# Group statistics by 32x32 transpositions and one aggregation on VectorE instead of two small TensorE products

## The chip, the cores and the metric

The kernel runs on one core of one Trainium2 chip. The metric is the device time of one execution in microseconds (us). Engines are named as in the profile: PE is TensorE's matrix product, PEld its weight load, DVE is VectorE, ACT is ScalarE, POOL is GpSimd, SP is SyncE (here it only issues transfers).

## The reference

An attention block over 16 images of 512 channels by 32x32 pixels, all in float32: a group normalisation, query, key and value products, softmax attention with four heads, an output product and the residual.

```python
b, c, h, w = x.shape                        # 16, 512, 32, 32
xg = x.reshape(b, NUM_GROUPS, -1)           # 8 groups of 64 channels
mu = jnp.mean(xg, axis=-1, keepdims=True)
var = jnp.var(xg, axis=-1, keepdims=True)
xn = ((xg - mu) * jax.lax.rsqrt(var + EPS)).reshape(b, c, h, w)
xn = xn * norm_gamma[:, None, None] + norm_beta[:, None, None]
qkv = jnp.einsum('oc,bchw->bohw', qkv_w, xn) + qkv_b[:, None, None]
q, k, v = jnp.split(qkv, 3, axis=1)         # then to 4 heads of 128
attn = jax.nn.softmax(jnp.einsum('bhnd,bhmd->bhnm', q, k) * scale, axis=-1)
out = jnp.einsum('bhnm,bhmd->bhnd', attn, v)
out = jnp.einsum('oc,bchw->bohw', proj_w, out) + proj_b[:, None, None]
return x + out
```

## The kernel before

Channels lie on the 128 partitions: an image is four tiles `x` (chunks c = 0 to 3) of 128 x 1024 numbers, and a group of 64 channels is half of the partitions of one chunk. The attention runs as one long sequence of steps, eight per head, four heads per image. In each step TensorE makes scores (L846, tile `s`), ScalarE their exponentials (L852, `p`), VectorE adds the exponentials up (L858, L860, `tot`), and TensorE makes the weighted sum of the step before (L942, `po`).

All other work is planned between these steps by `plan_head`, a list of units for each of the eight steps of a head: the query and key products of the next image, the value products, and the output product of the image before, all by Strassen's scheme on two levels (`strassen`, `two_levels`, tiles `qk_*`, `v_*`, `pp_*`). Its products go to PSUM banks x and y of the pool `ps_a`, two of each. Bank x is emptied by copies on ScalarE (L486, L628; `pp_p`, `pp_u`), bank y by additions on VectorE (L630; `pp_r`), and TensorE can only go on in a bank that has been emptied. Sums of inputs for the inner level are VectorE's (L574, `pp_t`; L319 for the image's own sums), as are the combinations of results (L679, 1024 wide), the residual additions (L826, L829, `y`) and the division by the softmax sum (L952). POOL issues the transfers of `x`, of the residual `y` and of the output `out_y` (L830). A scheduler puts the instructions of the units into one fixed order for each engine; `tc.issue_after` and `tc.high_priority(URGENT)` steer it.

The normalisation of image b + 1 is prepared while head 1 of image b runs. `load_x` brings the four chunks. `stats_chunk`, on ScalarE, makes the mean and the variance of each channel (columns 0 and 1 of `mv`). `stats_group` makes the statistics of the groups from these, four columns for the four chunks: a product with the matrix `avg` (blocks of 64 x 64 filled with 1/64) spreads the groups' mean of the channels' means over the partitions (L83, `pm`), VectorE makes the deviation's square and adds the variances, a second product spreads the group's variance (L88, `pv`), VectorE adds epsilon (L89, `ve`), POOL raises to the power -0.5 (L90, `rstd`), and VectorE multiplies by gamma and makes the shift (L76, L100, L102; `sc`, `t`, `sh`). The three parts are pinned behind the additions to `tot` of steps 2, 3 and 4 (3 for the first such image). Then `normalise` (L109 on ScalarE) scales and shifts the image in halves of a chunk. In PSUM `pm` and `pv` take a bank y each. Image 0 is prepared in `open_image`, in two pairs of chunks.

The tile with the tag `tt` has one buffer; the squares' output of `stats_chunk` (`junk`) and the transposed sums of `denominators` share it.

Of the kernel before, what the change touches and what calls it, by code (L numbers as in the profile page):

```python
# [10 lines left out]
F32 = mybir.dt.float32  # L11
I32 = mybir.dt.int32
AF = mybir.ActivationFunctionType
ALU = mybir.AluOpType
AX = mybir.AxisListType

P = 128
HEADS = 4
GROUPS = 8
EPS = 1e-5  # L20
BLK = 32
# [6 lines left out]
URGENT = 40  # L28
# [158 lines left out]
def fast_path(ctx, tc, x, sources, out, consts, flag, dims):  # L187
# [6 lines left out]
    nc = tc.nc  # L194
    B, C, N, NCC, NH2, NB, GC, SCALE = dims
    gamma, beta, qkv_wT, qk_b, v_b, proj_wT, proj_b = sources
    avg, neghalf, gamma_sb, beta_sb, qkb_sb, vb_sb, projb_sb = consts
# [4 lines left out]
    one = ctx.enter_context(tc.tile_pool(name="one", bufs=1))  # L202
# [8 lines left out]
    lpool = ctx.enter_context(tc.tile_pool(name="l", bufs=1))  # L211
    upool = ctx.enter_context(tc.tile_pool(name="u", bufs=2))
    ypool = ctx.enter_context(tc.tile_pool(name="y", bufs=4))
    gn = ctx.enter_context(tc.tile_pool(name="gn", bufs=2))
# [7 lines left out]
    spans = one.tile([BLK, B * HEADS - 1], F32, name="spans")  # L222
    ones = one.tile([BLK, 1], F32, name="ones")
    ones_sq = one.tile([P, P], F32, name="ones_sq")
    xs, xb, vs, qs, ks, os_, ob = {}, {}, {}, {}, {}, {}, {}
    mvs, scaled = {}, {}

# [20 lines left out]
        nc.vector.memset(avg[ts(g, GC), ts(g, GC)], 1.0 / GC)  # L248
    nc.vector.memset(neghalf, -0.5)
    nc.vector.memset(ones_sq, 1.0)  # L250
    for t, src in (
        (gamma_sb, gamma), (beta_sb, beta), (qkb_sb, qk_b), (vb_sb, v_b), (projb_sb, proj_b)
    ):
        nc.gpsimd.dma_start(t, src)

    norm = Norm(nc, gn, ps_a, avg, neghalf, gamma_sb, beta_sb, NCC, N, "y")

    def stats_chunk(b, c):
        if c == 0:
            mvs[b] = gn.tile([P, NCC, 2], F32, tag="mv", name=f"mv_{b}")  # L260

        junk = lpool.tile([P, N], F32, tag="tt", name=f"junk_{b}_{c}")
        sums = gn.tile([P, 3], F32, tag="st", name=f"sums_{b}_{c}")
        nc.scalar.activation(junk, xs[b, c], AF.Identity, accum_out=sums[:, 0:1])
        nc.scalar.mul(mvs[b][:, c, 0:1], sums[:, 0:1], 1.0 / N)
        nc.scalar.mul(sums[:, 1:2], sums[:, 0:1], -1.0 / N)
        nc.scalar.activation(
            junk, xs[b, c], AF.Square, bias=sums[:, 1:2], accum_out=sums[:, 2:3]
        )
        nc.scalar.mul(mvs[b][:, c, 1:2], sums[:, 2:3], 1.0 / N)  # L270

    def stats_group(b):


        g = []

        def part(n, first, last):
            if not g:
                g.extend(norm.group_steps(mvs[b]))
            with tc.issue_after(added[b - 1, 1, n].ins), tc.high_priority(URGENT):  # L280
                for step in g[first:last]:
                    step()

        def scale():
            n = 4 if b > 1 else 3
            part(n, 9, 10)
            with tc.issue_after(added[b - 1, 1, n].ins), tc.high_priority(URGENT):
                mu, sc = norm.result
                sh = norm.shift(mu, sc)
            for c in range(NCC):  # L290
                scaled[b, c] = sc, sh, c

        return [lambda: part(2, 0, 6), lambda: part(3, 6, 9), scale]

    def normalise(b, c, half, on_scalar=True):
        t = xs[b, c][:, ts(half, HALF)]
        sc, sh, i = scaled[b, c]
        return norm.apply(t, t, sc, sh, i, on_scalar)
# [16 lines left out]
    def sums_of_b(b, rows=(1, 2, 3), chunks=range(KC)):  # L315

        def sub(o, i, j):
            for k in chunks:
                nc.vector.tensor_sub(b[o][k], b[i][k], b[j][k])  # L319

        if 1 in rows:
            sub("t1", "b12", "b11")
        if 2 in rows:
            sub("t2", "b22", "t1")
        if 3 in rows:
            sub("t3", "t2", "b11")
            sub("t4", "b21", "t2")

    def x_sums(b, rows=(1, 2, 3)):
        if 1 in rows:  # L330
            xb[b] = halves([xs[b, c] for c in range(NCC)], "x")
        sums_of_b(xb[b], rows)

    def o_blocks(b):
        ob[b] = halves([os_[b, h] for h in range(HEADS)], "o")
# [33 lines left out]
    def stage_blocks(site):  # L369

        raw = raw_blocks(site)
        st = stage[site] = {}
        names = ("a11", "a12", "a21", "a22", "s1", "s2")
        if site in ("proj", "v"):
            for n in names[:4]:
                st[n] = ypool.tile([P, HALF], F32, tag="y", name=f"st_{n}")
            for i, n in enumerate(names[4:]):
                st[n] = tpool.tile([P, HALF], F32, tag=f"ot2{i}", name=f"st_{n}")
        else:
            for i in range(3):  # L380
                t = opool.tile([P, N], F32, tag="o", name=f"st_{site}_{i}")
                for h in range(2):
                    st[names[2 * i + h]] = t[:, ts(h, HALF)]
        for n in names[:4]:
            load_block(st[n].rearrange("p (s d) -> p s d", d=P), raw[n])
# [450 lines left out]
    inverse, rows_of, added, exps = {}, {}, {}, {}  # L836
    steps = B * HEADS * NB
# [116 lines left out]
    def spread(plan, units, first, last):  # L954

        for i, u in enumerate(units):
            plan[first + i * (last - first) // len(units)].append(u)
# [20 lines left out]
    def staggered(lists, starts=None):  # L978


        starts = starts or (0, 4, 8, 16)[: len(lists)]
        at = [(a + i, g, u) for g, (a, us) in enumerate(zip(starts, lists))
              for i, u in enumerate(us)]
        return [u for _, _, u in sorted(at, key=lambda t: t[:2])]
# [104 lines left out]
    def plan_head(b, h):  # L1089

        plan = [[] for _ in range(NB)]
        if h == 0:
            spread(plan, staggered(next_qk.pop()), 0, NB)
            if b > 0:
                plan[6].append(lambda: o_blocks(b - 1))
                plan[6].append(lambda: sums_of_b(ob[b - 1]))
            else:
                plan[5].append(lambda: stage_blocks("v"))
        elif h == 1:
            if b > 0:  # L1100
                spread(plan, staggered(proj_groups(b - 1)), 0, NB)
            if b + 1 == B:
                plan[0].append(lambda: last_loads("x"))
            else:
                plan[0].append(lambda: load_x(b + 1))
                spread(plan, [lambda c=c: stats_chunk(b + 1, c) for c in range(NCC)], 2, 4)
                sums, power, scale = stats_group(b + 1)
                if b == 0:

                    plan[4] += [sums, power, scale]  # L1110
                else:
                    plan[4].insert(0, sums)
                    plan[4].insert((len(plan[4]) + 1) // 2, power)
                    plan[5].insert(0, scale)
                for r in range(2):
                    plan[5 + r] += [

                        lambda c=c, half=half: normalise(b + 1, c, half, b > 0 or c % 2 == 1)
                        for c in range(KC * r, KC * r + KC) for half in range(NH2)
                    ]  # L1120
                plan[6].append(lambda: x_sums(b + 1, (1,)))
            if b == 0:
                for g in range(len(OUTER)):
                    plan[g // 2].append(lambda g=g: kept_group("v", g))
                    plan[NB // 2 - 1 + g].append(lambda g=g: kept_group("proj", g))
                plan[2].append(lambda: stage_blocks("proj"))
                spread(plan, [lambda o=o: bias_of_v(o) for o in range(NCC)], 3, 5)
        elif b + 1 == B:
            if h == 2:
                plan[0].append(lambda: last_loads("w"))  # L1130
                plan[2].append(last_bias)
            else:
                os_[b, h] = opool.tile([P, N], F32, tag="o", name=f"o_{b}_{h}")
                plan[3].append(lambda: o_blocks(b))
                plan[3].append(lambda: sums_of_b(ob[b], (1,)))
                plan[5].append(lambda: sums_of_b(ob[b], (2, 3), (0,)))
        elif h == 2:
            spread(plan, staggered(qk_groups(b + 1, 0)), 0, NB)

            plan[0].insert(2, lambda: x_sums(b + 1, (2,)))  # L1140
            plan[1].append(lambda: x_sums(b + 1, (3,)))
        else:

            spread(plan, staggered(next_v.pop()), 0, NB - 1)

            plan[NB - 2].append(lambda: ahead[f"qk_{b + 1}_1"]())
        return plan
# [92 lines left out]
    plan = []  # L1240
    for s in range(steps + 1):
        units = []
        if s < steps:
            b, h, j = where(s)
            if j == 0:
                plan = plan_head(b, h)
# [7 lines left out]
        for half in range(NH2):  # L1254
# [11 lines left out]
            n = (len(units) + 1) // 2  # L1266
# [137 lines left out]
```

## Time and profile before

| | |
|---|---|
| Median of three runs | 3172.76 us (3171.57 to 3177.14) |
| Profiled execution, span | 3170.7 us |
| Around the span, against the median | 2.1 us |
| Granted TensorE clock | 1.000 |
| PE, DVE, ACT, POOL busy | 3159.9, 2633.6, 1439.7, 517.7 us |
| `pm` and `pv`, 128x4 | 30 TensorE passes each (two for one float32 product) |
| Power on POOL (L90), 128x4 | 15, mean 1940 ns |

How to read it: a float32 product is two records (passes) of TensorE. A record's length exceeds the spacing of the starts since passes overlap, so lengths of time on TensorE are read from start to start. A line of the timeline gives start, length, engine, source line, operation, tiles, shapes and the number of instructions merged; in brackets stands the engine's idle time before it and what ended it. In a line of a group, the numbers after the count are the busy time in us and the mean of one in ns. The word "now" in the prediction means the kernel before.

### The profile page before, as it was taken

How to read it: one execution, taken by the hardware profiler on the slowest of the kernel's cores; microseconds unless marked ns; L12 is line 12 of the kernel's file. 1: busy time of each engine (PE TensorE's matmuls, PEld its weight loads, DVE VectorE, ACT ScalarE, POOL GpSimd, SP SyncE). 2: the span in 40 equal slices, each digit the busy share in tenths (PEclk: the TensorE clock that was granted, in tenths of full speed). 3: DMA queues.
4: the chain of work that ended last, by engine and by line, in shares of the span. 5: the costliest groups of instructions: out<-in, count | busy, mean ns of one | idle time of the engine just before them, and what ended most of it. 6: DMA issues, size and time to landing. Idle time of an engine off the chain costs nothing.

```text
span 3170.7 us, 34267 instructions
## 1 busy us (share of the span) xinstructions
PE 3159.9 (100%) x10524; PEld 2190.7 (69%) x10524; DVE 2633.6 (83%) x4639; ACT 1439.7 (45%) x2712; POOL 517.7 (16%) x898
## 2 busy tenths in 40 slices
PE   9999999999999999999999999999999999999999
PEld 7566676677766676777767767677676776766764
DVE  9878879788897888878788787987879978788784
ACT  3535435354353543545435453453534545344342
POOL 0011221111211112211122111222012221122200
PEclk9999999999999999999999999999999999999999
DMA  5554554555545455454554545555455564555531
GB/s 177 185 190 154 188 172 154 171 153 192 171 164 162 153 185 175 167 167 145 191 172 162 171 145 187 171 172 172 144 175 169 176 189 134 174 162 186 179 116 41
DMA packets 210333, 524.32 MB, mean 165 GB/s; under 512 B 32096, under 2 KB 65376, under 8 KB 210144
## 3 DMA queue, kind: packets, MB, share of 16 engines
q1 hardware_dynamic: 132896, 282.12, 28.8%
q0 software_dynamic: 64000, 204.54, 19.2%
q10 hardware_dynamic: 13248, 35.39, 3.5%
q8 instruction: 87, 1.43, 0.2%
q14 instruction: 102, 0.84, 0.1%
HBM read 388.77 MB, written 133.17 MB: 165 GB/s over the span
## 4 chain that ended last, share of the span: by engine, by line
PE 96%; DVE 3%; DMA 0%; issue 0%; POOL 0%; SPq 0%; ACT 0%; DVEq 0%; POOLq 0%
PE po L942 27%; PE s L846 27%; PE qk_x L606 12%; PE qk_y L606 9%; PE pp_x L606 6%; PE v_x L606 6%; PE pp_y L606 4%; PE v_y L606 4%; PE lx L1031 0%; DVE qk_t L574 0%; PE ly L1031 0%; PE warm L1153 0%; DVE tot L860 0%; DVE qk L714 0%; DVE qk_r L630 0%
## 5 line engine op out<-in xcount | busy, mean ns | idle before, releaser
L942 PE MATMUL po<-p,v 128*128 128x512 f32 x2048 | 1049.5, 594 | 0.7 <-ACT p L852 0.7
L846 PE MATMUL s<-qk,qk 128*128 128x512 f32 x2048 | 1047.4, 593 | 0.3 <-DVE qk L714 0.3
L852 ACT ACTIVATE p<-s 128x512 f32<-128x512 f32 x1024 | 610.9, 597 | 961.0 <-PE s L846 957.2
L942 PEld LDWEIGHTS po<-p,v 128*128 128x128 f32 x2048 | 603.6, 302 | 322.7 <-issue 214.5
L860 DVE TENSOR_TENSOR tot<-tot,p 128x1024 f32<-128x1024 f32 x385 | 469.0, 1218 | 158.4 <-ACT p L852 156.3
L846 PEld LDWEIGHTS s<-qk,qk 128*128 128x128 f32 x2048 | 387.7, 190 | 88.6 <-issue 29.9
L606 PEld LDWEIGHTS qk_x<-qk_t,w 128*128 128x128 f32 x1344 | 251.8, 190 | 166.1 <-issue 75.3
L606 PE MATMUL qk_x<-qk_t,w 128*128 128x256 f32 x1344 | 356.3, 382 | 0.1
L486 ACT COPY qk_u<-qk_x 128x512 f32<-128x512 f32 (+1 forms) x256 | 136.3, 533 | 229.2 <-PE qk_x L606 229.2
L779 POOL DMA_DIRECT2D vd<-vu x120 | 66.7, 557 | 899.8 <-DVE vu L771 897.9
L630 DVE TENSOR_TENSOR qk_r<-qk_y,qk_u 128x512 f32<-128x512 f32 (+1 forms) x256 | 157.7, 616 | 34.7 <-ACT qk_u L486 21.6
L580 POOL DMA_DIRECT2D kept_t<-qk_t x240 | 129.4, 540 | 278.4 <-DVE qk_t L574 211.9
L606 PEld LDWEIGHTS pp_x<-pp_t,w_proj 128*128 128x128 f32 x630 | 117.2, 190 | 74.7 <-issue 32.3
L784 POOL DMA_DIRECT2D v<-vd x240 | 140.6, 593 | 167.1 <-DMA vd<-vu 70.3
L630 DVE TENSOR_TENSOR v_r<-v_y,v_u 128x512 f32<-128x512 f32 (+1 forms) x120 | 76.0, 633 | 110.6 <-ACT v_u L486 80.3
L606 PE MATMUL pp_x<-pp_t,w_proj 128*128 128x256 f32 x630 | 167.8, 383 | 0.0
L606 PE MATMUL v_x<-v_t,w_v 128*128 128x256 f32 x630 | 166.6, 381 | 0.0
L830 POOL DMA_DIRECT2D out_y<-y x120 | 66.0, 550 | 604.2 <-DVE y L829 602.4
L606 PEld LDWEIGHTS v_x<-v_t,w_v 128*128 128x128 f32 x630 | 118.4, 190 | 55.3 <-issue 19.1
L606 PE MATMUL qk_y<-x,w 128*128 128x256 f32 x512 | 142.1, 379 | 0.0
L714 DVE SCALAR_TENSOR_TENSOR qk<-qk_r,qkb_sb,qk_r 128x512 f32<-128x512 f32 x192 | 137.5, 743 | 1.6
L486 ACT COPY v_u<-v_x 128x512 f32<-128x512 f32 (+1 forms) x124 | 66.3, 535 | 157.1 <-PE v_x L606 130.3
(217 smaller groups left out, 4487.2 us busy)
## 6 DMA issues: line engine op xcount, KB each, us to landing
w<-kept SPq DMA_DIRECT2D x90, 512.0 KB, 3.7
kept_t<-qk_t POOLq DMA_DIRECT2D x180, 256.0 KB, 3.3
v_t<-kept_t SPq DMA_DIRECT2D x180, 256.0 KB, 2.9
w<-kept SPq DMA_DIRECT2D x90, 384.0 KB, 3.4
rinv<-row ACTq DMA_DIRECT2D x63, 512.0 KB, 4.9
x<-in_x POOLq DMA_DIRECT2D x60, 512.0 KB, 4.6
vd<-vu POOLq DMA_DIRECT2D x120, 256.0 KB, 3.1
v<-vd POOLq DMA_DIRECT2D x240, 128.0 KB, 4.2
```

The costliest lines, as they stand in the source:

```text
L486: nc.scalar.copy(t[n][:, :width], t["x"][:, :width])
L580: nc.gpsimd.dma_start(t, to)
L606: nc.tensor.matmul(acc[:, ts(i, Q)], have["w"][t][:, i, slot, :], inner(i, bn), start=(first and i == 0), stop=True, skip_group_check=True,)
L630: nc.vector.tensor_add(dst, view(a), view(c))
L714: nc.vector.scalar_tensor_tensor(st[b, h][:, ts(half, HALF)], a, qkb_sb[:, i : i + 1], c, ALU.add, ALU.add)
L779: nc.gpsimd.dma_start(rows[which][ts(h, P), :], u)
L784: nc.gpsimd.dma_start(vs[b, pair][ts(q, BLK), half].rearrange("m h (k i) j -> m (h k) (i j)", k=n), rows[which].rearrange("(k m) (q e) -> ...
L830: nc.gpsimd.dma_start(out[b, ts(o, P), ts(half, HALF)], t)
L846: nc.tensor.matmul(sc, ks[b, h][:, ts(j, P)], qs[b, h][:, ts(half, HALF)], start=True, stop=True)
L852: exps[s] = nc.scalar.activation(ps[s][:, ts(half, HALF)], sc, AF.Exp, scale=SCALE)
L860: added[b, h, j] = nc.vector.tensor_add(tot[b, h][:, i], tot[b, h][:, i], ps[s][:, i])
L942: nc.tensor.matmul(po[b, h][:, i], v_block(b, h, j), ps[s][:, i], start=(j == 0), stop=(j == NB - 1),)
```

## The change

For images 1 to 15 the statistics of the channels go to the columns 0 to 3 of a `table` of 128 x 2 x 32, which is cleared once: the means, and the sums of squared deviations (so ScalarE's last scaling falls away). `stats_group` becomes one batch behind the add to `tot` of step 3: a transposition in 32x32 blocks brings the channels of a block of 32 partitions into a row, for each chunk; four copies bring in the neighbouring block's row, so that the 64 channels of a group stand side by side; `bn_aggr` makes mean and variance of the group from 64 triples of count, mean and sum; then epsilon, the power on POOL for one column, a transposition of the result, spread over 32 columns, back to the partitions, and `sc`, `t`, `sh` as before. Image 0 keeps the products. The scratch lies in the tile with the tag `tt`.

```diff
+    table = one.tile([P, 2, BLK], F32, name="table")
...
+    nc.gpsimd.memset(table, 0.0)
...
     def stats_chunk(b, c):
-        if c == 0:
-            mvs[b] = gn.tile([P, NCC, 2], F32, tag="mv", name=f"mv_{b}")
-
+        mean, spread_ = (
+            (mvs[b][:, c, 0:1], mvs[b][:, c, 1:2]) if b == 0
+            else (table[:, 0, c : c + 1], table[:, 1, c : c + 1])
+        )
...
-        nc.scalar.mul(mvs[b][:, c, 1:2], sums[:, 2:3], 1.0 / N)
+        if b == 0:
+            nc.scalar.mul(spread_, sums[:, 2:3], 1.0 / N)

     def stats_group(b):
-        g = []
-        def part(n, first, last):
-            if not g:
-                g.extend(norm.group_steps(mvs[b]))
-            with tc.issue_after(added[b - 1, 1, n].ins), tc.high_priority(URGENT):
-                for step in g[first:last]:
-                    step()
...
-        return [lambda: part(2, 0, 6), lambda: part(3, 6, 9), scale]
+        def steps():
+            t = lpool.tile([P, N], F32, tag="tt", name=f"groups_{b}")
+            rows = t[:, : 6 * BLK].rearrange("p (s j) -> p s j", s=3)
+            both = t[:, 6 * BLK : 6 * BLK + 2]
+            ve = t[:, 6 * BLK + 2 : 6 * BLK + 3]
+            back = t[:, 8 * BLK : 10 * BLK].rearrange("p (s j) -> p s j", s=2)
+            v.memset(rows[:, 0, :], float(N))
+            v.transpose(rows[:, 1:3, :BLK], table)
+            for q in range(quads):
+                v.tensor_copy(rows[ts(q, BLK), 1:3, BLK:], rows[ts(q ^ 1, BLK), 1:3, :BLK])
+            v.bn_aggr(both, rows.rearrange("p s j -> p j s"))
+            v.tensor_scalar_add(ve, both[:, 1:2], EPS)
+            nc.gpsimd.tensor_tensor(both[:, 1:2], ve, neghalf[:, 0:1], ALU.pow)
+            v.transpose(back, both.unsqueeze(2).to_broadcast([P, 2, BLK]))
+            sc = gn.tile([P, NCC], F32, tag="sc", name="sc")
+            v.tensor_mul(sc, back[:, 1, k], gamma_sb)
+            sh = norm.shift(back[:, 0, k], sc)
+            for c in range(NCC):
+                scaled[b, c] = sc, sh, c
+
+        def all_():
+            with tc.issue_after(added[b - 1, 1, 3].ins), tc.high_priority(URGENT):
+                steps()
+        return all_
...
-                sums, power, scale = stats_group(b + 1)
-                if b == 0:
-                    plan[4] += [sums, power, scale]
-                else:
-                    plan[4].insert(0, sums)
-                    plan[4].insert((len(plan[4]) + 1) // 2, power)
-                    plan[5].insert(0, scale)
+                plan[4].insert(0, stats_group(b + 1))
```

More of the change, by code (lines that the diff above doesn't have):

```diff
@@ L264, in stats_chunk @@
         nc.scalar.activation(junk, xs[b, c], AF.Identity, accum_out=sums[:, 0:1])
-        nc.scalar.mul(mvs[b][:, c, 0:1], sums[:, 0:1], 1.0 / N)
+        nc.scalar.mul(mean, sums[:, 0:1], 1.0 / N)
         nc.scalar.mul(sums[:, 1:2], sums[:, 0:1], -1.0 / N)
         nc.scalar.activation(
-            junk, xs[b, c], AF.Square, bias=sums[:, 1:2], accum_out=sums[:, 2:3]
-        )
-        nc.scalar.mul(mvs[b][:, c, 1:2], sums[:, 2:3], 1.0 / N)
+            junk, xs[b, c], AF.Square, bias=sums[:, 1:2],
+            accum_out=sums[:, 2:3] if b == 0 else spread_,
+        )
@@ L272, in stats_group @@
+        if b == 0:
+            nc.scalar.mul(spread_, sums[:, 2:3], 1.0 / N)
     def stats_group(b):
-        g = []
-        def part(n, first, last):
-            if not g:
-                g.extend(norm.group_steps(mvs[b]))
-            with tc.issue_after(added[b - 1, 1, n].ins), tc.high_priority(URGENT):
-                for step in g[first:last]:
-                    step()
[L284 to L289, printed above, removed]
+        v = nc.vector
@@ new lines, in stats_group @@
+        quads = P // BLK
+        k = slice(0, NCC)
+        def steps():
[15 more added lines that the diff above has]
+            sh = norm.shift(back[:, 0, k], sc)
```

## The prediction

> **What bounds it.** I read the page first, then the timeline around the two products. The line of busy times and the chain:
>
> ```profile
> PE 3159.9 (100%) x10524; PEld 2190.7 (69%) x10524; DVE 2633.6 (83%) x4639; ACT 1439.7 (45%) x2712; POOL 517.7 (16%) x898
> ...
> PE 96%; DVE 3%; DMA 0%; issue 0%; POOL 0%; SPq 0%; ACT 0%; DVEq 0%; POOLq 0%
> ```
>
> TensorE has no spare time: whatever it no longer does shortens the run, and whatever it newly waits for lengthens it. VectorE is only 83% busy, but it empties the banks that TensorE needs again, so its lateness counts in this stage. The timeline of PE there (image 2, prepared during image 1):
>
> ```profile
> 506.62 1.03 PE L606 MATMUL pp_x<-pp_t,w_proj 128*128 128x256 f32 x4
> 507.48 0.28 PE L83 MATMUL pm<-mean,avg 128*128 128x4 f32 x2
> 507.62 1.11 PE L606 MATMUL pp_x<-ot,w_proj 128*128 128x256 f32 x4
> 508.57 1.02 PE L846 MATMUL s<-qk,qk 128*128 128x512 f32 x2
> ...
> 514.17 0.59 PE L606 MATMUL pp_y<-ot,w_proj 128*128 128x256 f32 x2
> 514.69 0.39 PE L88 MATMUL pv<-vv,avg 128*128 128x4 f32 x2
> 514.93 1.10 PE L846 MATMUL s<-qk,qk 128*128 128x512 f32 x2
> 515.87 1.02 PE L942 MATMUL po<-p,v 128*128 128x512 f32 x2
> ```
>
> **Removed from TensorE.** A pass of 256 columns starts every 0.215 us, one of 512 every 0.43. `pm` takes 0.14 (507.48 to 507.62), and the four passes behind it 0.95 instead of 0.86: 0.23. `pv` starts 0.09 after 514.17 + 0.43, holds 0.24, and its follower loses another 0.08: 0.42 (rounded times; 0.66 for both). Fourteen images repeat this: 9.2 us. For image 1 PE also waits 1.36 us ahead of `pm`; 1.36 + 0.33 + 0.34 = 2.0. So 11.3 us at most. ScalarE loses four scalings of 0.2 us (L270) per image, worth nothing at 45% busy. The table's one MEMSET on POOL lies in the opening, ahead of small loads, and is taken at nothing (under 0.25 us).
>
> **Added to VectorE, in the built order.** For images 2 to 15 the new block starts behind the add to `tot` of step 3 (L860), as one batch with other work between its steps: memset, transposition, a `pp_t` difference, four copies, another difference, `bn_aggr`, the residual add to `y_1_0` (L829), `ve`, an eviction (L630), the transposition that waits for POOL, the next eviction, `sc`, L829, product `t`, a 1024-wide add (L679), `sh`. The rows that price it:
>
> ```profile
> L52 DVE BATCH_NORM_AGGREGATE mv<-st 128x2 f32<-128x12 f32 x3 | 0.6, 209 | 0.1
> L877 DVE STREAM_TRANSPOSE l<-l 32x32 f32<-32x32 f32 x63 | 12.2, 194 | 0.6
> ```
>
> *Aggregation* of 192 numbers (64 triples). The row has 12 numbers, four triples, in 209 ns; a VectorE operation on four numbers takes 152 (L89). If the extra 57 ns go by triple, 64 cost 0.91 + 0.15 = 1.06 us; if they are a fixed end, 0.21 + 180 at about 1 ns = 0.40. I take 1.06: the row exceeds the floor by seven times what its 8 further numbers explain. *Transpositions* of 64 columns: 0.194 plus 32 columns at 1.05 ns (1.230 us for 1024 at L869), 0.23 each. *Memset*: 0.11 by 64x64 at L248. *Copies*: 0.18 (a 32x32 add) to 0.215, I take 0.19 each. They read and write different groups of 32 partitions, and the row for that is
>
> ```profile
> 545.82 0.18 DVE L874 TENSOR_TENSOR l<-part 32x32 f32<-32x32 f32 x1
> 546.02 0.18 DVE L875 TENSOR_TENSOR l<-part 32x32 f32<-32x32 f32 x1
> 546.23 0.43 DVE L574 TENSOR_TENSOR qk_t<-xt 128x256 f32<-128x256 f32 x1
> ```
>
> where each starts 0.02 to 0.03 behind the end of the one before, while equal-based VectorE work starts 0.08 ahead of it (L679 at 516.14, the next at 517.28). So four copies take 4 x 0.21 = 0.84; overlapping they would take 0.45, and the sum would be 14 x 0.39 = 5.5 us lower. [...]
>
> *Power on POOL*, which VectorE now waits for with two evictions queued behind it. Of L90, the opening and image 2:
>
> ```profile
> 9.44 0.68 DVE L49 BATCH_NORM_STATS2 st<-x 128x6 f32<-128x512 f32 x1
> 9.61 0.72 POOL L90 TENSOR_TENSOR rstd<-ve,neghalf 128x2 f32<-128x2 f32 x1 [5.49 <-DVE ve L89]
> 14.99 0.68 DVE L1171 TENSOR_TENSOR x<-x 128x512 f32<-128x512 f32 x1
> 15.15 1.08 POOL L90 TENSOR_TENSOR rstd<-ve,neghalf 128x2 f32<-128x2 f32 x1 [4.81 <-DVE ve L89]
> ...
> 516.14 1.22 DVE L679 TENSOR_TENSOR pp_r<-pp_r,pp_r 128x1024 f32<-128x1024 f32 x1
> 516.19 2.06 POOL L90 TENSOR_TENSOR rstd<-ve,neghalf 128x4 f32<-128x4 f32 x1
> ```
>
> Under an operation with one input in SBUF two columns take 0.72. Under one with two, they end 0.56 after that operation, and four columns 0.90 after it (518.25 against 517.36). So 2.06 is mostly waiting for L679, a column costs 0.17, and one column unhindered 0.72 - 0.17, some 0.56. In the new order the power starts under L630, whose other input is PSUM; I take 0.56, bounds 0.39 (another 0.17 less) and 2.06 (as now). [...]
>
> **The sum for one image**, on the clock of image 2. The `tot` add starts at 510.02 (510.26 less `pm`); the block follows at 511.16. Transposition to 511.42, `pp_t` to 511.76, copies to 512.60, `pp_t` from 512.58, aggregation 512.92 to 513.98, L829 513.90 to 514.59 (now 512.76). POOL issues `out_y` 0.29 later, for 0.55, and the power runs 515.45 to 516.00. (The load of `y` behind it is issued some 2 us later than at 515.64; its reader, L826, comes after 526, so that is covered.) The transposition starts at 516.04, the second eviction at 516.19 (now 514.80). Then L829, `t`, L679 and `sh` at their present spacing: `sh` ends at 518.88. That is 2 us earlier than now (520.98), but the built ScalarE queue has moved too: in it the four normalisations L109 of x_0 and x_1 and an exponential stand ahead of the second copy `pp_u` that empties bank x, which in the kernel before stands ahead of all of them. Four times 0.70, 0.50 and 0.59 behind `sh`: `pp_u` ends at 522.82, PE goes on at 522.88. Without a wait it would at 522.09 (521.90 less 0.66, plus one `po` of 0.86 that the new order puts ahead). Its next bank, y, is emptied by an L630 that stands behind L860, L952, L679 (1.14 each), two `pp_t` (0.34) and one x sum (0.60) behind `sh`: 523.49 to 524.17, PE at 524.22 instead of 522.95. So PE loses 1.27 us and wins 0.66: 0.61 per image, 8.5 for fourteen. The exposed weight load that goes with the first wait costs 0.08 (1.11 against 1.03 in the passes behind it) and exists now too, so it cancels:
>
> ```profile
> 521.88 0.73 PEld L606 LDWEIGHTS pp_x<-pp_t,w_proj 128*128 128x128 f32 x4 [0.65 <-ACT pp_u L486]
> 521.90 1.11 PE L606 MATMUL pp_x<-pp_t,w_proj 128*128 128x256 f32 x4
> ```
>
> Image 1 has another neighbourhood (weights being made); its 2.0 may be won or as much lost again, I take nothing. The span is 3170.7; the three runs lie around 3172.76, 2.1 above it, which does not change: 3172.76 + 8.5, 3181.
>
> **Rivals.** (1) *The aggregation costs 0.40.* All that follows is 0.66 earlier, PE loses 0.61 and wins 0.66: level, 3172. For: 12 numbers are few to tell a slope. Against: what the fixed end would be. (2) *The lateness stays off PE*: the other side, one mechanism. If the chain from the `tot` add to the y eviction is shorter by 1.22 us (aggregation 0.40, power 0.39, copies overlapping: 0.66 + 0.17 + 0.39), that eviction meets 522.95 almost, and PE keeps what it no longer does: 3162. It tells as faster from 1.06 us on, where 0.45 per image is won; at 0.61 it is level. For: VectorE idles 2 us between 509.7 and 514.8, room for the block. Against: the added idle time lies behind that room, at the wait for POOL. (3) *The power keeps 2.06 us* because it stands behind a DMA issue, as L813 stands now: 1.5 more per image, 21, 3202. Against: the ends above follow VectorE, not the DMA. (4) That the products stay: the built PE order has them only in the opening, so not.
>
> **Numbers.** My case 0.52, (1) 0.24, (2) in whole or most 0.12, (3) 0.07, something else longer (a second aggregation pass, image 1) 0.05. A change under about 0.2% (6.3 us) can hardly be told by runs that spread over 5.6. My case with copies at 0.215 (1.4 us), power at 0.9 (4.8) and image 1 at a loss of 2 gives 3190; case (1) with a power of 0.39 (2.4 less) and image 1 at a gain of 2 gives 3168. Range 3168 to 3190. Slower by over 0.2% (above 3179.1): 0.50 of my case, (3) and the rest, 0.62; same: (1), 0.02 of my case and 0.01 of (2), 0.27; faster: the other 0.11 of (2).
>
> **What would show it.** No `pm` or `pv` rows but the opening's; `bn_aggr` with 192 inputs near 1.06; copies starting behind each other's end; the power near 0.56 with VectorE idle about 0.7 ahead of the second transposition; PE waits of 0.79 and 0.4 at `pp_x` and `pp_y` 14 times, released by ACT `pp_u` and DVE L630. An aggregation under 0.5, or no such waits, makes me wrong.

## The result, and the profile after

| | before | after |
|---|---|---|
| Median | 3172.49 us (3171.36 to 3177.14, 12 runs) | 3180.52 us (3179.14 to 3182.95, 12 runs) |
| Span of the profiled execution | 3170.7 us | 3178.9 us |

The ratio is 1.0025, with an interval of 1.0018 to 1.0032: slower by 8.0 us. The forecast was 3181. That the two are so close is partly luck: terms of its sum were off and nearly cancelled. It also left unsaid what the runs below show, that the place of the new block costs more than its arithmetic saves.

The page of the kernel after, busy times and chain. Behind `stats_group` its line numbers are 15 higher than before (L606 is L621, L630 is L645, L486 is L501), and the new steps are L290 to L299:

```profile
PE 3157.6 (99%) x10464; PEld 2187.1 (69%) x10464; DVE 2655.3 (84%) x4684; ACT 1436.6 (45%) x2652; POOL 500.0 (16%) x899
...
PE 68%; issue 23%; DVE 7%; POOL 1%; DMA 1%; ACT 0%; SPq 0%; ACTq 0%; POOLq 0%; DVEq 0%
```

TensorE has 60 passes fewer and is busy 2.3 us less, in a span that is 8.2 us longer: it waits. The chain, which ran along TensorE almost alone (96%), now crosses to VectorE and POOL; the 23% of issue is time for which the profile shows no cause, so its shares are no prices. The waits of TensorE that come once per image (view of waits: total, times, longest) are

```profile
PE pp_x L621 <- ACT pp_u L501: 6.3, 14, 0.5
PE pp_y L621 <- DVE pp_r L645: 3.3, 14, 0.2
```

Neither was in the kernel before. The view counts from the modelled end of a record; from start to start they are 0.61 and 0.40 us. The timeline of image 2, all engines:

```profile
513.62 0.19 DVE L291 STREAM_TRANSPOSE groups<-table 128x64 f32<-128x64 f32 x1
...
514.12 0.79 DVE L293 COPY groups<-groups 32x64 f32<-32x64 f32 x4
...
515.28 1.01 DVE L294 BATCH_NORM_AGGREGATE groups<-groups 128x2 f32<-128x192 f32 x1
...
517.13 0.55 POOL L845 DMA_DIRECT2D out_y<-y  x1 [28.75 <-DVE groups L295]
...
517.70 0.57 POOL L296 TENSOR_TENSOR groups<-groups,neghalf 128x1 f32<-128x1 f32 x1
...
518.30 0.24 DVE L297 STREAM_TRANSPOSE groups<-groups 128x64 f32<-128x64 f32 x1 [0.81 <-POOL groups L296]
...
520.98 0.15 DVE L102 TENSOR_TENSOR sh<-beta_sb,t 128x4 f32<-128x4 f32 x1
...
521.17 1.52 ACT L109 ACTIVATE x<-x,sh,sc 128x512 f32<-128x512 f32 x2 [1.05 <-DVE sh L102]
...
523.07 1.51 ACT L109 ACTIVATE x<-x,sh,sc 128x512 f32<-128x512 f32 x2
...
524.48 0.57 ACT L501 COPY pp_u<-pp_x 128x512 f32<-128x512 f32 x1
...
525.10 1.13 PE L621 MATMUL pp_x<-pp_t,w_proj 128*128 128x256 f32 x4 [0.45 <-ACT pp_u L501]
...
525.73 0.69 DVE L645 TENSOR_TENSOR pp_r<-pp_y,pp_u 128x512 f32<-128x512 f32 x1
...
526.47 0.70 PE L621 MATMUL pp_y<-ot,w_proj 128*128 128x256 f32 x2 [0.24 <-DVE pp_r L645]
```

Read it downwards: the block on VectorE, the power on POOL behind a transfer's issue, VectorE idle for 0.81 us, `sh`, four normalisations on ScalarE, only then the copy `pp_u` that empties bank x, and TensorE behind it; then bank y, which VectorE empties from 525.73 to 526.42. In the kernel before, `sh` stands at nearly the same time, but the scores of this stage are 2.15 us earlier there (511.16 against 513.31), so measured from them `sh` came later; the copy stood ahead of the normalisations:

```profile
520.83 0.15 DVE L102 TENSOR_TENSOR sh<-beta_sb,t 128x4 f32<-128x4 f32 x1
...
521.24 0.59 ACT L486 COPY pp_u<-pp_x 128x512 f32<-128x512 f32 x1 [1.12 <-PE pp_x L606]
...
521.72 0.82 ACT L109 ACTIVATE x<-x,sh,sc 128x512 f32<-128x512 f32 x1
...
521.90 0.68 DVE L630 TENSOR_TENSOR pp_r<-pp_y,pp_u 128x512 f32<-128x512 f32 x1
```

To see where the loss sits, I compared the start of every score product with the same one of the kernel before. The difference grows by 0.47 us per image for images 2 to 15 (6.5 us) and by 1.1 through image 1; 0.8 is there from the opening, where the difference lies between -0.2 and +0.8 in the profiled executions of these kernels. The table gives these two growths for every kernel that follows, each from its one profiled execution; the waits are from start to start and the same to 0.02 us in all 14 images, but for what is said of `z_copies`.

| Kernel | Median, us | Ratio to before (95%) | us per image, 2 to 15 | Image 1, us | TensorE's waits per image |
|---|---|---|---|---|---|
| after | 3180.5 | 1.0018 to 1.0032 | +0.47 | +1.1 | `pp_x` 0.61, `pp_y` 0.40 |
| `a_twice` | 3186.2 | 1.0032 to 1.0059 | +0.88 | +1.4 | `pp_x` 1.03, `pp_y` 0.40 |
| `d_nopow` | 3174.0 | 0.9997 to 1.0015 | +0.08 | -0.6 | `pp_x` 0.73 |
| `c_prod_batch` | 3185.7 | 1.0030 to 1.0057 | +0.85 | +1.6 | `pp_x` 0.46, `pp_y` 0.25, a `po` 0.20 |
| `b_pins` | 3165.1 | 0.9967 to 0.9986 | -0.65 | +2.6 | none |
| `x_late_scale` | 3170.9 | 0.9988 to 1.0006 | -0.26 | +0.8 | a later `pp_y` 0.20 |
| `y_early_sums` | 3187.5 | 1.0036 to 1.0063 | +1.02 | +0.4 | `pp_x` 0.49 and 0.55, `pp_y` 0.42 |
| `z_copies` | 3189.4 | 1.0039 to 1.0067 | +1.21 | +0.7 | `pp_y` 1.61 |
| `b_twice` | 3171.7 | 0.9988 to 1.0006 | -0.28 | +3.9 | a later `pp_y` 0.21 |
| `after_img1` | 3178.7 | 1.0011 to 1.0029 | +0.46 | -0.3 | as after |
| `best` | 3163.5 | 0.9962 to 0.9983 | -0.65 | +0.2 | none |

Before, in the same comparisons, had medians of 3172.2 to 3172.3.

### The profile page after: what moved, and what is told of

It reads as the page before. It is cut to its first block, busy times and chain, and to the rows that moved or that the text cites. A ratio compares the mean times of both kernels' runs of the same rounds, so it can differ in the third digit from the quotient of the medians.

```text
span 3178.9 us, 34101 instructions
## 1 busy us (share of the span) xinstructions
PE 3157.6 (99%) x10464; PEld 2187.1 (69%) x10464; DVE 2655.3 (84%) x4684; ACT 1436.6 (45%) x2652; POOL 500.0 (16%) x899
## 4 chain that ended last, share of the span: by engine, by line
PE 68%; issue 23%; DVE 7%; POOL 1%; DMA 1%; ACT 0%; SPq 0%; ACTq 0%; POOLq 0%; DVEq 0%
PE po L957 19%; PE s L861 19%; PE qk_x L621 9%; PE qk_y L621 7%; PE v_x L621 6%; PE v_y L621 4%; PE pp_y L621 1%; PE pp_x L621 1%; DVE pp_r L694 1%; DVE o L967 1%; DVE qk_t L589 1%; DVE qk_r L645 1%; DVE tot L875 1%; DVE pp_r L645 1%; DVE qk_r L694 0%
## 5 line engine op out<-in xcount | busy, mean ns | idle before, releaser
L875 DVE TENSOR_TENSOR tot<-tot,p 128x1024 f32<-128x1024 f32 x385 | 470.4, 1222 | 165.9 <-ACT p L867 165.9
L621 PEld LDWEIGHTS qk_x<-qk_t,w 128*128 128x128 f32 x1344 | 251.7, 190 | 166.7 <-issue 75.3
L621 PE MATMUL qk_x<-qk_t,w 128*128 128x256 f32 x1344 | 356.5, 382 | 0.1
L501 ACT COPY qk_u<-qk_x 128x512 f32<-128x512 f32 (+1 forms) x256 | 136.3, 533 | 230.0 <-PE qk_x L621 230.0
L645 DVE TENSOR_TENSOR qk_r<-qk_y,qk_u 128x512 f32<-128x512 f32 (+1 forms) x256 | 158.2, 618 | 34.8 <-ACT qk_u L501 21.6
L621 PE MATMUL pp_x<-pp_t,w_proj 128*128 128x256 f32 x630 | 168.1, 383 | 6.3 <-ACT pp_u L501 6.3
L621 PEld LDWEIGHTS pp_x<-pp_t,w_proj 128*128 128x128 f32 x630 | 117.2, 190 | 75.9 <-ACT pp_u L501 26.7
L645 DVE TENSOR_TENSOR v_r<-v_y,v_u 128x512 f32<-128x512 f32 (+1 forms) x120 | 76.7, 639 | 110.4 <-ACT v_u L501 80.1
L621 PE MATMUL v_x<-v_t,w_v 128*128 128x256 f32 x630 | 166.6, 381 | 0.0
L621 PEld LDWEIGHTS v_x<-v_t,w_v 128*128 128x128 f32 x630 | 118.4, 190 | 55.3 <-issue 19.1
L621 PE MATMUL qk_y<-x,w 128*128 128x256 f32 x512 | 142.1, 379 | 0.0
L786 DVE STREAM_TRANSPOSE vu<-vt 128x512 f32<-128x512 f32 x120 | 135.9, 1133 | 2.4 <-DMA vd<-vu 2.3
```

The costliest lines, as they stand in the source:

```text
L501: nc.scalar.copy(t[n][:, :width], t["x"][:, :width])
L621: nc.tensor.matmul(acc[:, ts(i, Q)], have["w"][t][:, i, slot, :], inner(i, bn), start=(first and i == 0), stop=True, skip_group_check=True,)
L645: nc.vector.tensor_add(dst, view(a), view(c))
L786: nc.vector.transpose(u.rearrange("p (q i j) -> p j q i", q=n, i=BLK), t.rearrange("p (j q i) -> p j q i", q=n, i=BLK),)
L875: added[b, h, j] = nc.vector.tensor_add(tot[b, h][:, i], tot[b, h][:, i], ps[s][:, i])
```

## The experiments

**More of it, and less.** `a_twice` and `d_nopow` change one cost inside the block of the kernel after, each in a kernel of its own:

```diff
             v.bn_aggr(both, rows.rearrange("p s j -> p j s"))
+            v.bn_aggr(both, rows.rearrange("p s j -> p j s"))   # a_twice
...
-            nc.gpsimd.tensor_tensor(both[:, 1:2], ve, neghalf[:, 0:1], ALU.pow)
+            v.reciprocal(both[:, 1:2], ve)                       # d_nopow
```

> Kernel after with the aggregation issued twice (same operands, same result), a dose of one more 1.015 us on VectorE inside the block, 15 times; the built orders of VectorE, ScalarE and TensorE hardly move. Theory A (the block's length on VectorE reaches TensorE through the two bank evictions, `pp_u` behind the normalisations that wait for `sh`, and L645 behind the block): TensorE's two waits per image, 0.63 and 0.40 us in after, together grow by 0.9 to 1.0, so 3180.5 + 14 x 0.95 = 3194 (image 1 up to 1 more). Theory B (the loss is elsewhere, in the opening and in image 1, and VectorE's slack takes the block): under 3183.

> Kernel after with a VectorE reciprocal in place of the power on POOL: it leaves out the square root, so the images but the first are scaled by 1/(var+eps) instead of its root. VectorE no longer waits for POOL (0.81 us per image); the reciprocal adds about 0.15. Theory A: the block ends 0.6 to 0.7 us earlier, TensorE's two waits fall from 0.63 and 0.40 to about 0 and 0: 3180.5 - 14 x 0.6 to 0.9 = 3168 to 3172. Theory B: 3179 to 3181.

The dose cost 5.7 us, 0.42 per image, where 0.95 was expected. The timeline of `a_twice` says why:

```profile
516.87 0.55 POOL L846 DMA_DIRECT2D out_y<-y  x1 [28.75 <-DVE y L845]
...
517.86 0.56 POOL L297 TENSOR_TENSOR groups<-groups,neghalf 128x1 f32<-128x1 f32 x1 [0.44 <-DVE groups L296]
...
518.46 0.24 DVE L298 STREAM_TRANSPOSE groups<-groups 128x64 f32<-128x64 f32 x1 [0.17 <-POOL groups L297]
```

In the kernel after the power stands in POOL's queue behind the issue of `out_y` (517.13 + 0.55), and VectorE waits 0.81. With 1.0 us more in front of `ve` the issue is over before `ve` comes, the power starts at once, and the wait shrinks to 0.17. So the block grew by 1.01 - 0.64 = 0.37, and TensorE's wait at `pp_x` by 0.42, nearly one for one. The mechanism of theory A holds; its size was off by more than half, because the expectation had left POOL's queue out. Theory B, under 3183, falls.

Without the power the block is 0.81 - 0.16 = 0.65 us shorter, and 6.5 us come back, to 3174.0 where 3168 to 3172 was expected. The wait at `pp_y` is gone, but not the one at `pp_x`, which was expected to go. The built orders moved with this edit: on VectorE a residual addition (L844) and an add 1024 wide (L694), which stand ahead of `sh` in after, now stand behind it, so `sh` came 2.25 us earlier, measured from the same score product; and on ScalarE six halves of normalisations (L109), not four, then stood ahead of the second `pp_u`. So this run is not a pure change of one cost. It fits that what the shorter block wins is partly lost again by ScalarE's order.

**The place alone, and the arithmetic alone.** `c_prod_batch` is the kernel before, its three parts run as one batch behind step 3. `b_pins` is the kernel after, its block cut into the three parts that the kernel before had:

```diff
-            with tc.issue_after(added[b - 1, 1, 3].ins), tc.high_priority(URGENT):
-                steps()
+        return pinned(2, sums), pinned(3, power), pinned(4 if b > 1 else 3, scale)
...
-                plan[4].insert(0, stats_group(b + 1))
+                    plan[4].insert(0, sums)
+                    plan[4].insert((len(plan[4]) + 1) // 2, power)
+                    plan[5].insert(0, scale)
```

> The arithmetic of the kernel before (two products on TensorE), but all its steps in one batch behind step 3, where the kernel after has its block. Rival D (the place alone costs, whatever is computed): TensorE keeps 0.66 us per image of products and gets the waits of after, 1.15: 3172.5 + 14 x 1.15 = 3189 or more, since the batch now also crosses from VectorE to TensorE and back twice. Theory A in its strict form (VectorE's 1.0 of aggregation and 0.8 of copies are needed for the lateness): the products' small VectorE steps are about 1.5 us shorter than the new ones, but two crossings are added; waits of at most 0.4 per image: 3172.5 to 3178.

> The arithmetic of the kernel after, but cut in three parts that are issued behind steps 2, 3 and 4 of the attention, at the places that the three parts of the kernel before had; so other VectorE work lies between the power on POOL and the transposition that reads it, and ScalarE copies both banks out ahead of the normalisations. Theory A (lateness of the block, put in one batch, is what costs): no waits of TensorE at `pp_x` and `pp_y` but the exposed weight load of 0.09; the products stay away: 3180.5 - 14 x (1.24 - 0.09) = 3164, or 3172.5 - 14 x 0.66 = 3163 counted from before. Rival C (the arithmetic's own VectorE time, 3.7 us per image, costs wherever it stands): 3178 to 3181. Theory B (opening and image 1): both stay as they are in after, their 1.9 us too, and the rest is as in A: 3164 to 3166.

With before and after these make a square:

| | three parts behind steps 2, 3, 4 | one batch behind step 3 |
|---|---|---|
| two products on TensorE | 3172.2 | 3185.7 |
| transpositions and aggregation | 3165.1 | 3180.5 |

In either place the new arithmetic is faster, by 7.1 and by 5.2 us; with either arithmetic the batch is slower, by 13.5 and by 15.4. The slowdown is that of the place, with the orders that the scheduler builds for it. Rival D comes nearest for `c_prod_batch`, 3185.7 where it had 3189 or more; the place also shows in that kernel's own chain, where VectorE idles 0.68 us for `pv` and 1.22 for the power, and in the kernel before for neither. Per image the three parts give -0.65, all of the 0.66 that the prediction read off `pm` and `pv`. `b_pins` lies just above theory A's 3163 to 3164 and within theory B's 3164 to 3166, which lets image 1 keep its loss; it does (+2.6 in the table). Rival C in full falls, and so does theory A's strict form: the products, whose small VectorE steps are some 1.5 us shorter, are late in a batch as well.

**Which cut matters.** The block has two ends that could be moved apart from each other. `x_late_scale` leaves memset to power behind step 3 and moves the rest behind step 4; `y_early_sums` moves memset to aggregation behind step 2 and leaves the rest behind step 3. Shown against `b_pins`, from which each differs in this line alone:

```diff
-        return pinned(2, sums), pinned(3, power), pinned(4 if b > 1 else 3, scale)   # b_pins
+        return pinned(3, sums), pinned(3, power), pinned(4 if b > 1 else 3, scale)   # x_late_scale
+        return pinned(2, sums), pinned(3, power), pinned(3, scale)                   # y_early_sums
```

> Kernel after with its batch cut in one place: memset to power stay behind step 3, and the transposition, `sc`, `t` and `sh` are issued behind step 4 (as the last part of the kernel before). Aggregation and copies stand where they stand in after; VectorE's wait for POOL is covered by other work, `sh` comes later, and ScalarE copies both banks out first. If these two (the wait and the early `sh`) are what costs, both waits of TensorE go: 3180.5 - 14 x 1.1 = 3164 to 3166, as with the three parts. If the aggregation's place behind step 3 is already too late, the eviction of bank y is still late by about 0.4 after a TensorE that comes 0.6 earlier: 3171 to 3174.

> The other cut: memset to aggregation are issued behind step 2, and power, transposition, `sc`, `t`, `sh` in one batch behind step 3, so the wait for POOL stays and `sh` comes some 3 us earlier than in after. In the built ScalarE order six halves of normalisations stand ahead of the first copy `pp_u` out of bank x and all eight ahead of the second. If the aggregation's place is the larger part of the loss: 3164 to 3168. If the early `sh` and what it lets ScalarE do first is the larger part (the cut at the other place won 9.6 us): the eviction of bank y comes in time, the copies of bank x do not, some 0.3 to 0.7 us per image as with the reciprocal: 3170 to 3176.

Moving the end of the block to later won 9.6 us; moving its beginning to earlier lost 7.0 when the end stayed, and won 5.8 (3170.9 to 3165.1) when the end had been moved. With the beginning at step 2, the place of the end alone is worth 22.4 (3187.5 against 3165.1). `x_late_scale` came out between its two expectations, by the second: the two waits went, and 0.20 us and an exposed weight load (0.11) appeared at a later product in bank y, where VectorE is still behind.

The surprise is `y_early_sums`, which I had put at 3176 at most. The timeline of its ScalarE and VectorE, and VectorE's waits:

```profile
515.93 2.93 ACT L109 ACTIVATE x<-x,sh,sc 128x512 f32<-128x512 f32 x4 [2.09 <-DVE sh L102]
518.77 0.58 ACT L878 ACTIVATE p<-s 128x512 f32<-128x512 f32 x1
519.25 1.51 ACT L109 ACTIVATE x<-x,sh,sc 128x512 f32<-128x512 f32 x2
520.66 0.57 ACT L512 COPY pp_u<-pp_x 128x512 f32<-128x512 f32 x1
```

```profile
517.49 0.69 DVE L345 TENSOR_TENSOR x<-x 128x512 f32<-128x512 f32 x1 [0.99 <-ACT x L109]
```

```profile
DVE x L345 <- ACT x L109: 13.8, 14, 1.0
```

`sh` is ready at 515.9, 3.7 us after the scores at 512.19 (7.8 in the kernel after, 9.8 before). ScalarE then runs six halves of normalisations before the first copy out of bank x, and VectorE, in its fixed order, now has an input sum of the next image (L345) ahead of an eviction (L656, 518.10) and idles 0.99 us for it. In `b_pins`, with `sh` 6.6 us later from the same score product, TensorE waits for nothing in this stage: nothing there needs the statistics yet. When they come early, what they release stands, in the built orders, ahead of the copies and evictions that TensorE needs.

**ScalarE's order alone.** `z_copies` keeps the block of after and puts the normalisations of images 2 to 15 behind the copies:

```diff
+        if b > 1:
+            with tc.issue_after(copied[-1].ins):    # the last copy pp_u
+                return norm.apply(t, t, sc, sh, i, on_scalar)
```

> Kernel after, with one order edge on ScalarE for images 2 to 15: the normalisations L109 stand behind the last copy `pp_u` that was written before them, so both copies out of bank x run ahead of them, as in the kernel before. The block on VectorE, its wait for POOL and the place of `sh` are those of after. If ScalarE's queue alone makes TensorE wait (theory A1), both waits go: 3180.5 - 14 x 1.15 = 3164. If the two evictions are late for reasons of their own (theory A2), the wait at `pp_x` goes and the one at `pp_y` grows, since TensorE comes to it 0.61 us earlier while VectorE's eviction is only some 0.3 earlier (in the built order an L841 of 0.66 stands ahead of it instead of an x sum and a `pp_t`, 0.94): 0.40 + 0.61 - 0.28, some 0.7 us, and 0.4 to 0.5 per image is won: 3174.

It has the highest median of all. (Of its 1.21 per image, 0.08 is one wait of 1.1 us for another bank in a single image.) Timeline:

```profile
522.19 0.59 ACT L506 COPY pp_u<-pp_x 128x512 f32<-128x512 f32 x1 [1.12 <-PE pp_x L626]
...
522.85 1.11 PE L626 MATMUL pp_x<-pp_t,w_proj 128*128 128x256 f32 x4
...
524.67 0.68 DVE L650 TENSOR_TENSOR pp_r<-pp_y,pp_u 128x512 f32<-128x512 f32 x1
...
525.40 1.13 PE L626 MATMUL pp_y<-ot,w_proj 128*128 128x256 f32 x4 [1.44 <-DVE pp_r L650]
...
526.37 1.04 PE L962 MATMUL po<-p,v 128*128 128x512 f32 x2
```

The copy is in time and the wait at `pp_x` is gone, so A1 had the release right; but the eviction of bank y, 0.3 earlier than in after, ends at 525.35 only, and TensorE waits 1.61 us for it. Theory A2 had 0.7. What it missed is that the built order of TensorE also moved: a `po` of 0.86 us that ran ahead of `pp_y` now stands behind it and can't fill the wait: 0.40 + 0.61 - 0.28 + 0.86 = 1.59. So the two waits of the kernel after lie one behind the other but are not one: the first is made by the time of `sh` and ScalarE's order together, and goes with the order; the second is VectorE's lateness in this stage, which the first had partly covered. Measured from the start of the score product that stands at 511.16 before (513.31 in after), the eviction of bank y starts 10.7 us later in before, 10.9 in `b_pins`, 11.3 in `x_late_scale`, 12.1 in `z_copies`, 12.4 in after. `x_late_scale` and `z_copies` both copy first; the 0.8 between them is as much as VectorE's wait for POOL, 0.81, which `x_late_scale` does not have.

**Is VectorE's time free in the three parts?** `b_twice` repeats the dose there.

> The three parts (3165.1), with the aggregation issued twice: the same dose of 1.0 us on VectorE that cost the single batch 0.4 us per image. If VectorE's time is hidden in that place (theory A): 3165 to 3167. If it costs wherever it stands (theory C): 3171 to 3179.

It cost 6.6 us: 0.38 per image, and 1.2 in image 1. The expectation by theory A fails, and 3171.7 lies at the lower end of theory C's: the three parts have room for the new steps, but less than 1.0 us more, and what is over costs. The wait it makes is that of `x_late_scale`, 0.21 at the later product in bank y.

**Image 1.** `after_img1` is the kernel after with the old products for image 1 alone, `best` the three parts for images 2 to 15 and the old products for image 1:

```diff
     def stats_group(b):
+        if b == 1:
+            return stats_group_1(b)      # the two products, in three parts
```

> Kernel after, with the two products and three parts of the kernel before for image 1 only; images 2 to 15 as in after. If the 2 us that after lost against before between 120 and 165 us come from the new steps: 3180.5 - 2 = 3178.5, and the starts of the scores stand level with those of before at 330 us, but for what the opening shows. If not: 3180.5.

> The three parts for images 2 to 15, and for image 1, where the new steps lost 4.2 us between 120 and 165 us, the two products as in the kernel before. From the spans: 3165.1 - 4.2 = 3161 if image 1 goes as before; 3165 if its loss is not from the new steps.

`after_img1` came where it was expected, 1.9 us under after. `best` gained 1.6 us on `b_pins`, between its two expectations: the 4.2 had counted only the stretch after the 1.6 us that image 1 first saves without its products; over both, the traces show 2.6 less 0.2. That is more than the medians' 1.6; the profiled execution of `b_pins` was the slowest of its ten (3166.4), and 1.7 of its 2.6 is a stretch at half clock, told in the last section. The trace of after shows what image 1 pays there: TensorE no longer waits 1.36 for `pm`, but 1.3 at small products `pb`, 1.4 at a `po` whose copy stands behind normalisations, and 0.5 more for weights at 159 us. `best` beats both kernels: 8.7 us under before, by the ratio 0.9962 to 0.9983. Its timeline, at the place where the kernel after waits twice:

```profile
520.33 1.02 PE L897 MATMUL s<-qk,qk 128*128 128x512 f32 x2
521.19 1.11 PE L657 MATMUL pp_x<-pp_t,w_proj 128*128 128x256 f32 x4
522.14 1.03 PE L993 MATMUL po<-p,v 128*128 128x512 f32 x2
523.01 1.03 PE L657 MATMUL pp_y<-ot,w_proj 128*128 128x256 f32 x4
```

Each start follows the one before by the spacing of its passes, but for the 0.09 of a weight load behind `pp_x`, which the kernel before has too. What would gain more in this stage is not to be found in TensorE's waits.

## Why the prediction was right, and where it was not

- *Removed from TensorE, 0.66 per image.* Right: the kernels without a wait keep 0.65.
- *Prices on VectorE and POOL.* Aggregation 1.06 forecast, 1.015 measured, near the price by triple and far from the 0.40 of a fixed end; four copies 0.84, measured 0.79, each starting 0.013 to 0.014 behind the end of the one before; transpositions 0.23, measured 0.19 and 0.25; memset 0.11 as forecast; power 0.56, measured 0.567 in 13 of 15 images and 0.582 in one, all started while VectorE ran nothing. In image 1 it took 1.43 (137.48 to 138.90), started under an addition with two inputs in SBUF (L875, 137.25 to 138.47), and ended 0.43 after it; in the kernel before two and four columns of L90 ended 0.56 and 0.90 after such an operation.
- *VectorE idle about 0.7 at the second transposition.* 0.81, with the cause that was named, POOL's issue of `out_y` in front of the power. `a_twice` confirmed it by accident.
- *The two waits.* 0.79 at `pp_x` by ACT `pp_u` and 0.4 at `pp_y` by DVE L645: 0.61 and 0.40, with these releasers, 14 times. The first was too large by 0.18. Of this, 0.15 is that the copy `pp_u` ended 12.65 us after the start of the `tot` add, not 12.80: the four copies, the aggregation and the residual addition behind it were each 0.05 to 0.06 shorter than summed.
- *The exposed weight load cancels.* Wrong twice, both small. The sum doesn't do what it says: its loss of 1.27 is 0.08 more than its two waits, 0.79 + 0.40, because the time without a wait, 522.95, is 522.09 + 0.86 and leaves the load out, while the times with waits hold it. And the load doesn't cancel: after a wait it is 0.107, and there are two of them, against one of 0.087, which adds 0.13 per image. So from the forecast's 0.61 go 0.18 and 0.08, and 0.13 comes on: 0.61 + 0.40 + 0.13 - 0.66 = 0.48, and the score starts show 0.47. Over 14 images that is 6.5 us instead of 8.5.
- *Image 1 at nothing.* Wrong by 1.1 us in the trace and 1.9 in the medians (`after_img1`). This and the 2.0 us above are about equal and opposite, which is why 3181 met 3180.5. That is luck.
- *The rivals.* (1) and (3) fall with the measured aggregation and power. (2), that TensorE keeps what it saves, is not what after does, but its mechanism is real: `best` is it, at 3163.5 where (2) had 3162. The condition that I gave for it was too narrow. I asked that the chain be 1.22 us shorter; the runs show that the same steps, no shorter, do it from other places. (4) had been excluded by the built order.
- *What the account lacked.* The prediction put the lateness down to the length of the chain on VectorE. The square shows that the old steps in the same place lose 13.5 us as well. And it read the queue behind the earlier `sh` (2 us; measured 2.0) from the built order without counting the early `sh` itself as a cost; `y_early_sums` against `b_pins` shows that it is one, in the orders that the scheduler builds.

## What to carry to other kernels

Where engines run in fixed orders and one of them has no spare time, change what is computed and where it is issued in separate kernels: here the arithmetic won 5 to 7 us and the place lost 13 to 15. Here the small chain with a hop to another engine ran best when it was cut at the hop, with other work between the parts, and when its last step, which releases much work, came late. Two waits that lie one behind the other on the bound engine have to be priced together: here taking away the first alone made the second 1.2 us longer, 0.86 of it because TensorE's order moved too.

## What the chip showed that I had not expected

In image 1 of the profiled execution of `b_pins` TensorE waits twice, 0.98 us up to 158.28 and 1.73 up to 160.95 (for weights), and then runs at half rate: passes of 256 columns start every 0.43 instead of 0.215 us. View of windows of `b_pins`, then of `c_prod_batch` (length, PE busy, weight load, DVE, ACT, POOL, granted clock, DMA share, GB/s):

```profile
158.00:161.00 3.00, 1.15 (x5) 0.75 (x5) 3.00 (x9) 0.59 (x1) 1.08 (x2) 0.98 0.97 276
161.00:164.40 3.40, 3.40 (x9) 2.75 (x10) 0.93 (x2) 1.08 (x2) 0.00 (x0) 0.52 0.91 326
```

```profile
158.00:161.00 3.00, 1.22 (x6) 1.12 (x7) 2.26 (x5) 0.08 (x1) 0.00 (x0) 1.00 0.94 274
161.00:164.40 3.40, 3.40 (x18) 2.99 (x17) 1.58 (x3) 1.62 (x4) 0.00 (x0) 1.00 0.48 189
```

The clock granted is 0.52 for 3.4 us, at a cost of 1.7 us (six spacings 0.214 too long, and 0.38 at the ends). `c_prod_batch` is hardly busier in the same 3 us (1.22 against 1.15), waits 2.97 us in one piece, and keeps its clock, granted at 1.00 in both windows.

`b_twice` has such a stretch too: its granted clock is 1.00 from 154.00 to 161.00, 0.77 from 161.00 to 164.40 and 0.74 from 164.40 to 168.00, which makes some 3.4 us at half clock. These are the 3.4 us just before the two stretches, of `b_pins` and `b_twice`:

```profile
157.45:160.86 3.41, 1.12 (x5) 0.68 (x4) 3.41 (x11) 0.59 (x1) 1.08 (x2) 1.00 0.95 276
159.44:162.86 3.42, 1.39 (x7) 1.26 (x8) 2.17 (x6) 0.26 (x2) 0.00 (x0) 1.00 0.93 321
```

TensorE was not idle in them: it was busy for 1.12 and 1.39 us. Nor is so little work enough by itself. The wait of `c_prod_batch`, 2.8 us from the modelled end of the record before it, lies between 154.00 and 161.00 us, so 3.4 us that hold it have some 0.6 us of work, and the granted clock is 1.00 there and up to 168.00. What decides when the clock falls is not shown by these runs.
